# One scan over four rows instead of four scans: a change to the state-space stage of a macaron kernel

## The chip, the cores and the metric

The kernel runs on one core of one Trainium2 chip. The core has five engines that run side by side and meet at semaphores: TensorE (PE in the profile, its weight loads PEld), VectorE (DVE), ScalarE (ACT), GpSimd (POOL) and SyncE (SP), which here issues the DMAs. SBUF and PSUM are the on-chip memories, and all tiles here lie over up to 128 partitions. The kernel uses PSUM in banks of 512 fp32 per partition; TensorE's results go there, and no instruction of GpSimd in this kernel has an operand in it. The metric is the device time of one execution in microseconds.

## The reference

A macaron block over 2048 tokens of 128 features:

```
x = x + 0.5 * ffn(layernorm(x))
x = x + attn(layernorm(x))        # a state-space layer, in spite of its name
x = x + 0.5 * ffn(layernorm(x))
```

`ffn` is itself six layers, each of windowed attention (16 heads of 64, window 32) and a gated feed-forward part; it runs twice, with the same weights. The change lies in the middle line. There, with 256 channels d and 16 states n per channel,

```
delta = softplus(dt @ dt_w + dt_b)
dA  = exp(delta[l, d] * A[d, n])
dBu = (delta * u)[l, d] * B[l, n]
s   = dA[l] * s + dBu[l]            # in order of the tokens l, from s = 0
y[l, d] = sum over n of s[d, n] * C[l, n]
```

All data are fp32.

## The kernel before

The kernel works on the transposed activations, features on partitions. The attention layers go tile by tile (128 tokens), two segments of 1024 tokens, six layers, then the second run of `ffn`. The order of the instructions on each engine is written out by hand: `ORDER` gives for each stage of a tile a lag in steps and a place within the step, and `run` emits all the stages of a step in order of their place. Every engine executes its instructions in that order and waits where a semaphore is not yet there.

The state-space layer lies beside the attention tiles, from about 850 to 2550 us. It goes by pieces of 256 tokens (`SUB`), eight in all, one every 12 steps (`ROUND`), which is some 217 us. Its stages and their times in steps after the piece's start are listed in `SPACE`. Channels take two groups c of 128 partitions, and the 16 states n are taken in eight pairs q of two states j each, n = 2q + j. What runs per pair is

- `broadcast` (L1022): a DMA that spreads the rows of B and C of the two states over all partitions (tile `bc`);
- `source` (L1029): POOL computes `s` = B times delta u, in two instructions, one for each state (two SBUF inputs each, L1034);
- `decay` (L1039): ACT computes four exponentials of 256 elements into `da`, a tile of two PSUM banks laid out as [partition, j, c, 256 tokens] (L1044);
- `scan` (L1049): DVE runs four scans of 256 elements, one for each j and c, in place in `da`, with `da` as the factor, `s` as the addend and one column of `carry` as the initial value (L1055);
- `carried` (L1064): ACT copies the last column of each of the four rows into `carry`, for the next piece (L1066);
- `observe` (L1072): DVE multiplies `da` by C into `sc` (L1076);
- `gather` (L1084): PE adds the two rows of `sc` onto `y_ps` (L1089).

`s` and `bc` have two buffers each. `da` takes one of three pairs of PSUM banks that the attention tiles use too (`bank2`), from `decay` until `carried` and `observe` have both read it. `self.k.zero` (L1253 and L1254) is a column of zeros in SBUF, and `self.sp` the SBUF pool of this layer.

DVE's order around a scan is that of the tiles in the same step. The scans of a piece's first pair, for instance, are followed on DVE by the row sums of the softmax and their reciprocal (L546, L547), for which POOL's division L551 waits. Other stages that the text below names are the rotation on POOL (L408 adds two whole tiles, L440 multiplies a tile by a norm that is repeated over 64 elements), POOL's update of the activations of the piece before (L996), and small or plain DVE rows: L259 (a sum of 4 elements, one operand in PSUM), L631 (a memset of one column), L893 and L993 (256 elements, one operand in PSUM; L893 with a scalar for each partition).

Of the kernel before, what the change touches and what calls it, by code (L numbers as in the profile page):

```python
# [9 lines left out]
F32 = mybir.dt.float32  # L10
BF16 = mybir.dt.bfloat16
AF = mybir.ActivationFunctionType
ALU = mybir.AluOpType
# [4 lines left out]
P = 128  # L18
# [102 lines left out]
class Stream:  # L121
# [926 lines left out]

    def scan(self, b, s, q):  # L1049

        da = getattr(b, f"da{q}")
        for j in range(2):
            for c in range(2):
                n = 2 * q + j
                self.nc.vector.tensor_tensor_scan(  # L1055
                    da[:, j, c],
                    da[:, j, c],
                    getattr(b, f"s{q}")[:, j, c],
                    self.carry[:, c, n : n + 1],
                    ALU.mult,  # L1060
                    ALU.add,
                )

    def carried(self, b, s, q):  # L1064

# [312 lines left out]
```

## Time and profile before

| what | us |
|---|---|
| median of 3 runs | 3321.47 (3318.79 to 3322.2) |
| the profiled execution's own time | 3318.65 |
| its span in the profile | 3316.7 |
| PE busy | 3207.2 (97%) |
| POOL busy | 2907.3 (88%) |
| DVE busy | 2802.8 (85%) |
| ACT busy | 2551.6 (77%) |
| the 256 scans (L1055), all on DVE | 193.2 |

The mean granted clock of TensorE is 0.996. A row of the profile names a line of the kernel, the engine and operation, what is written and read, the shapes, how often, the busy time in us and the mean duration in ns, then how long the engine stood idle just before, and what ended most of that. In a timeline, a row has its start in us from the start of the span, its length in us, and in brackets an idle time ahead of it. The chain of waits is found backwards from the last instruction: at every step to what released it, or to the instruction before it on its engine.

### The profile page before, as it was taken

How to read it: one execution, taken by the hardware profiler on the slowest of the kernel's cores; microseconds unless marked ns; L12 is line 12 of the kernel's file. 1: busy time of each engine (PE TensorE's matmuls, PEld its weight loads, DVE VectorE, ACT ScalarE, POOL GpSimd, SP SyncE). 2: the span in 40 equal slices, each digit the busy share in tenths (PEclk: the TensorE clock that was granted, in tenths of full speed). 3: DMA queues.
4: the chain of work that ended last, by engine and by line, in shares of the span. 5: the costliest groups of instructions: out<-in, count | busy, mean ns of one | idle time of the engine just before them, and what ended most of it. 6: DMA issues, size and time to landing. Idle time of an engine off the chain costs nothing.

```text
span 3316.7 us, 97481 instructions
## 1 busy us (share of the span) xinstructions
PE 3207.2 (97%) x41936; PEld 2225.6 (67%) x41936; DVE 2802.8 (85%) x3540; ACT 2551.6 (77%) x4121; POOL 2907.3 (88%) x2317
## 2 busy tenths in 40 slices
PE   7999999999999999999999999999999999999997
PEld 4677677676666666666666666666666676777765
DVE  5778888887898989889989889898988888888884
ACT  6777777778778778787787877877777777777775
POOL 6999999998988989889888898898988888988983
PEclk9999999999999999999999999999999999999999
DMA  8222221221211122121211122111121111111000
GB/s 259 76 67 65 66 67 58 71 68 45 59 52 43 47 53 56 50 61 37 56 51 54 47 53 57 42 52 53 52 63 39 31 41 44 32 36 43 20 11 9
DMA packets 134494, 181.26 MB, mean 55 GB/s; under 512 B 13176, under 2 KB 91312, under 8 KB 127152
## 3 DMA queue, kind: packets, MB, share of 16 engines
q1 hardware_dynamic: 134064, 175.04, 18.0%
q8 instruction: 330, 5.41, 0.7%
q14 instruction: 100, 0.82, 0.1%
HBM read 138.75 MB, written 24.05 MB: 49 GB/s over the span
## 4 chain that ended last, share of the span: by engine, by line
PE 69%; DVE 12%; ACT 9%; POOL 7%; issue 2%; DMA 0%; SPq 0%; POOLq 0%; DVEq 0%; ACTq 0%
PE x_ps L372 16%; PE y_ps L617 16%; PE z_ps L596 8%; PE t_ps L453 8%; PE s_ps L511 6%; PE g_ps L698 3%; PE o_ps L744 3%; PE a_ps L698 3%; DVE da L1055 2%; DVE rot L391 2%; POOL rot L440 2%; DVE t L398 2%; PE y_ps L1089 2%; ACT da L1044 1%; ACT sq L384 1%
## 5 line engine op out<-in xcount | busy, mean ns | idle before, releaser
L408 POOL TENSOR_TENSOR rot<-rot,t 128x1024 f32<-128x1024 f32 x384 | 900.7, 2368 | 10.6 <-DVE rot L391 6.1
L372 PE MATMUL x_ps<-qk,r 128*128 128x512 f32 x1536 | 753.4, 613 | 29.6 <-ACT zt L608 10.1
L617 PEld LDWEIGHTS y_ps<-zt,m 128*128 128x128 f32 x6144 | 715.1, 192 | 63.8 <-ACT xc L667 36.6
L440 POOL TENSOR_TENSOR rot<-rot,rn 128x1024 f32<-128x1024 f32 x384 | 722.4, 1902 | 14.4
L617 PE MATMUL y_ps<-zt,m 128*128 128x128 f32 x6144 | 718.6, 275 | 5.3 <-ACT xc L667 3.1
L384 ACT ACTIVATE sq<-x_ps 128x1024 f32<-128x1024 f32 x384 | 393.2, 1024 | 276.3 <-DVE rot L391 229.9
L398 DVE TENSOR_TENSOR t<-x_ps,tab 128x1024 f32<-128x1024 f32 x384 | 467.7, 1218 | 154.6 <-PE i_ps L568 84.4
L551 POOL TENSOR_TENSOR pr<-pr,rs 128x1024 f32<-128x1024 f32 x192 | 365.2, 1902 | 198.8 <-DVE rs L547 174.0
L372 PEld LDWEIGHTS x_ps<-qk,r 128*128 128x128 f32 x1536 | 271.7, 190 | 361.8 <-issue 232.8
L391 DVE TENSOR_TENSOR rot<-x_ps,tab 128x1024 f32<-128x1024 f32 x384 | 467.3, 1217 | 20.0 <-ACT sq L384 19.5
L608 ACT COPY zt<-z_ps 128x1024 f32<-128x1024 f32 x384 | 368.9, 1010 | 140.8 <-PE z_ps L596 140.6
L414 DVE TENSOR_REDUCE ss<-sq 128x16 f32<-128x1024 f32 x384 | 466.5, 1215 | 7.7 <-ACT sq L384 5.0
L596 PE MATMUL z_ps<-pt,xw 32*128 32x512 f32 x3072 | 402.5, 614 | 3.1 <-DVE t L398 1.4
L535 POOL TENSOR_TENSOR pr<-pr,mx 128x1024 f32<-128x1024 f32 x192 | 365.3, 1903 | 25.9 <-ACT carry L1066 19.4
L453 PE MATMUL t_ps<-cs,rot 128*128 128x128 f32 x3072 | 370.9, 273 | 4.3 <-DVE sc L1076 2.1
L453 PEld LDWEIGHTS t_ps<-cs,rot 128*128 128x128 f32 x3072 | 344.1, 141 | 32.7 <-issue 9.8
L511 PE MATMUL s_ps<-kt,qt 64*32 64x64 f32 x24576 | 287.3, 225 | 0.5 <-issue 0.5
L511 PEld LDWEIGHTS s_ps<-kt,qt 64*32 64x32 f32 x24576 | 255.9, 105 | 47.1 <-issue 46.0
L541 ACT ACTIVATE pr<-pr 128x1024 f32<-128x1024 f32 x192 | 203.2, 1058 | 106.9 <-POOL pr L535 106.1
L596 PEld LDWEIGHTS z_ps<-pt,xw 32*128 32x128 f32 x3072 | 146.6, 184 | 163.4 <-issue 129.6
L561 DVE STREAM_TRANSPOSE pt<-pr 128x1024 f32<-128x1024 f32 x192 | 237.0, 1234 | 2.3 <-POOL pr L551 2.3
L546 DVE TENSOR_REDUCE rs<-pr 128x16 f32<-128x1024 f32 x192 | 232.9, 1213 | 6.2 <-ACT pr L541 3.3
(144 smaller groups left out, 4809.0 us busy)
## 6 DMA issues: line engine op xcount, KB each, us to landing
bc<-bc SPq DMA_DIRECT2D x64, 512.0 KB, 5.4
tab<-tab SPq DMA_DIRECT2D x120, 256.0 KB, 2.6
qk<-in_wqk_dram SPq DMA_DIRECT2D x24, 1024.0 KB, 5.0
m<-m SPq DMA_DIRECT2D x24, 1024.0 KB, 5.3
tab<-in_tabs_dram SPq DMA_DIRECT2D x48, 256.0 KB, 2.9
xw<-xw SPq DMA_DIRECT2D x192, 48.0 KB, 3.3
m<-mst SPq DMA_DIRECT2D x6, 1024.0 KB
w<-w1s SPq DMA_DIRECT2D x18, 341.0 KB, 3.5
```

The lines of the kernel that those rows point to most:

```text
L372: nc.tensor.matmul(out=x[:, j], lhsT=self.columns(g), rhs=st.w.qk[:, bass.ds(kind * INNER + j * 512, 512)], start=True, stop=True,)
L384: self.nc.scalar.activation(st.sq[kind], st.x[kind], AF.Square)
L391: self.nc.vector.tensor_tensor(st.rot[kind], st.x[kind], cos, ALU.mult)
L398: self.nc.vector.tensor_tensor(st.t2[kind].rearrange("p h (two c) -> p h two c", two=2), st.x[kind].rearrange("p h (two c) -> p h two c", ...
L408: self.nc.gpsimd.tensor_tensor(st.rot[kind], st.rot[kind], st.t2[kind], ALU.add)
L414: self.nc.vector.tensor_reduce(st.ss[:, kind, :], st.sq[kind], AX.X, ALU.add)
L440: self.nc.gpsimd.tensor_tensor(st.rot[kind], st.rot[kind], st.rn[:, kind, :].unsqueeze(2).to_broadcast([P, HEADS, DH]), ALU.mult,)
L453: self.nc.tensor.transpose(t_ps[:, c, :], flat[:, bass.ts(c, P)], self.k.ident)
L511: nc.tensor.matmul(out=st.s[32 * b : 32 * b + 32, par, c, :], lhsT=st.qt[rows, c, bass.ts(b, WIN)], rhs=st.kt[rows, c, bass.ds(WIN * b, 2 ...
L596: self.nc.tensor.matmul(out=st.z[b // 2][:, b % 2].rearrange("p (h q) -> p h q", q=WIN), lhsT=st.xw[rows, j, :], rhs=st.pt[rows, :, j, :], ...
L608: self.nc.scalar.copy(st.zt[:, 2 * half : 2 * half + 2].rearrange("p b h q -> p b (h q)"), st.z[half])
L617: self.nc.tensor.matmul(out=st.y_ps.rearrange("p (b q) -> p b q", q=WIN), lhsT=st.w.m[:, h // 2, h % 2, :], rhs=st.zt[:, :, h, :], start=( ...
```

## The change

`scan` computes the same states with one scan over all four rows of the pair, 1024 elements laid end to end. So that no row runs on into the next, the first column of `da` (the four decays at the first token of each row) is multiplied by the carry into a small new tile (4 elements per partition), that product is added to the first column of the source `s`, and the first column of `da` is set to zero; the scan then takes a constant zero as its initial value. All four instructions are DVE's, where the four scans stood. The sum into the source has both of its inputs in SBUF, `s` and the small tile; the product has one in PSUM and one in SBUF. On the other engines the instructions and their order are the same. In place of the waits of the four scans (the first and the third each waited for one half of the source from POOL, the first for the decays from ACT), the product waits for the decays, and the sum for both halves of the source.

```diff
     def scan(self, b, s, q):
 
-        da = getattr(b, f"da{q}")
-        for j in range(2):
-            for c in range(2):
-                n = 2 * q + j
-                self.nc.vector.tensor_tensor_scan(
-                    da[:, j, c],
-                    da[:, j, c],
-                    getattr(b, f"s{q}")[:, j, c],
-                    self.carry[:, c, n : n + 1],
-                    ALU.mult,
-                    ALU.add,
-                )
+
+        nc, da, src = self.nc, getattr(b, f"da{q}"), getattr(b, f"s{q}")
+        first, tmp = da[:, :, :, 0], self.sp.tile([P, 2, 2], F32, tag="s0", name="s0")
+        carry = self.carry[:, :, 2 * q : 2 * q + 2].rearrange("p c j -> p j c")
+        nc.vector.tensor_tensor(tmp, first, carry, ALU.mult)
+        nc.vector.tensor_tensor(src[:, :, :, 0], src[:, :, :, 0], tmp, ALU.add)
+        nc.vector.memset(first, 0.0)
+        flat = da.rearrange("p j c t -> p (j c t)")
+        nc.vector.tensor_tensor_scan(
+            flat, flat, src.rearrange("p j c t -> p (j c t)"), self.k.zero, ALU.mult, ALU.add
+        )
```

## The prediction

> **What bounds the kernel now.** First the page's busy shares and its chain, then busy time by stretch, then the chain of waits within the stretch that holds the scans, then the rows that give prices, last the timeline around single scans.
>
> ```profile
> PE 3207.2 (97%) x41936; PEld 2225.6 (67%) x41936; DVE 2802.8 (85%) x3540; ACT 2551.6 (77%) x4121; POOL 2907.3 (88%) x2317
> PE 69%; DVE 12%; ACT 9%; POOL 7%; issue 2%; DMA 0%; SPq 0%; POOLq 0%; DVEq 0%; ACTq 0%
> ...
> 850.00:2550.00 1700.00, 1646.15 (x20661) 1121.60 (x20660) 1524.77 (x1934) 1348.77 (x2253) 1513.85 (x1209) 1.00 0.19 51
> ```
>
> TensorE (PE) bounds the whole. All scans lie between 857 and 2542 us, so the third line (length, then busy PE, PEld, DVE, ACT, POOL) is the one to reason with: in 1700 us PE idles 54 us, DVE 175 us, POOL 186 us. No change to DVE can gain more than those 54 us. But PE there waits now and then for chains that run through DVE:
>
> ```profile
> by line: PE x_ps L372 13.5%; PE y_ps L617 11.2%; PE z_ps L596 6.4%; PE t_ps L453 6.0%; DVE da L1055 4.5%; PE s_ps L511 4.2%; PE y_ps L1089 3.0%; DVE rot L391 3.0%; issue 2.9%; DVE t L398 2.9%; ACT da L1044 2.7%; DVE ss L414 2.3%; POOL rot L
> ```
>
> 4.5% of 1700 us is 76.9 us of scans on the chain that ended last. Counting its pieces by pair, 26 of the 64 pairs of states are on it. With a pair called by its place q = 0 to 7 in its piece of 256 tokens: six of place 0, five of place 1, four of place 2, seven of place 3, two of place 5 and one each of places 6 and 7. The other 38 pairs have slack.
>
> **What goes.** The four scans of each pair.
>
> ```profile
> L1055 DVE TENSOR_TENSOR_SCAN da<-da,carry,s 128x256 f32<-128x256 f32 x256 | 193.2, 755 | 12.1 <-POOL s L1034 1.8
> L1076 DVE TENSOR_TENSOR sc<-da,bc 128x1024 f32<-128x1024 f32 x64 | 78.2, 1222 | 3.2 <-PE y_ps L1089 1.4 <-issue 0.2
> L893 DVE SCALAR_TENSOR_TENSOR u<-u_ps,pv,u 128x256 f32<-128x256 f32 x48 | 22.5, 482 | 7.7 <-ACT u L881 6.6
> L993 DVE TENSOR_TENSOR xm<-o_ps,xm 128x256 f32<-128x256 f32 x8 | 3.4, 424 | 0.2
> L259 DVE TENSOR_TENSOR b<-b_ps,pv 128x4 f32<-128x4 f32 x6 | 1.0, 163 | 9.5 <-PE b_ps L248 9.5
> L631 DVE MEMSET r<- 64x1 f32 x12 | 0.7, 59 | 0.7
> ...
> 1074.02 3.21 DVE L1055 TENSOR_TENSOR_SCAN da<-da,carry,s 128x256 f32<-128x256 f32 x4 [0.23 <-POOL s L1034]
> 1077.14 1.19 DVE L546 TENSOR_REDUCE rs<-pr 128x16 f32<-128x1024 f32 x1
> ...
> 1092.83 3.19 DVE L1055 TENSOR_TENSOR_SCAN da<-da,carry,s 128x256 f32<-128x256 f32 x4
> 1095.93 0.96 DVE L758 SCALAR_TENSOR_TENSOR r<-o_ps,pv,r 64x256 f32<-64x256 f32 x2
> ```
>
> From the first scan's start to the next instruction's start DVE is taken 3.12 and 3.10 us in these two; the mean of all 64 in the timeline is 3.08 us.
>
> **What comes, without any new wait.** The long scan: two-tensor rows of 256 and 1024 elements (424 and 1222 ns) give 1.04 ns per element and 158 ns fixed; a per-partition scalar adds 58 (482 against 424). The scan has one, so 216 of its 755 ns are fixed and 539 are 256 elements, 2.11 ns each. 1024 elements: 216 + 2156 = 2.37 us. Its scalar is now a constant zero, also a pointer, so the 216 stay. Product of first decay and carry (PSUM by SBUF, 4 elements): 0.16 by L259. Sum into the source: 0.16, the same row. The zeroing: 0.06 by L631; 0.16 if PSUM makes it cost what L259 does, nothing if it runs under the sum. Two waits on DVE's own semaphore at 0.03 each (1198.06 + 1.22 to 1199.31 from L546 to L547 in the timeline). The next instruction starts 0.09 before the scan's end, as now. Together 0.16 + 0.03 + 0.16 + 0.06 + 0.03 + 2.37 - 0.09 = 2.72, so 0.36 us less per pair (0.26 to 0.42).
>
> **A wait that is moved forward.** Now the third scan alone needs the second half of the source; the sum, which stands ahead of the whole long scan, will need both. Place 0 pays: POOL writes both halves from 1072.71 to 1075.21, DVE starts its scan at 1074.02, when the first is done. The sum can start at 1075.24, and the next instruction at 1075.24 + 0.16 + 0.06 + 0.03 + 2.37 - 0.09 = 1077.77 instead of 1077.14: 0.63 us more, in 7 of the 8 pieces (in the last, POOL ends 0.09 after the scan's start, and the pair gains like the others). Behind it on DVE stand the row sums L546 and L547, which POOL's L551 waits for, and then the product L1076 that PE's L1089 waits for. In the other 56 pairs both halves are done 0.35 us or more before the scan starts, and all four decays of ACT end ahead of the first scan in all 64, so the waits for whole tiles cost nothing there. The carry is 200 us old. No queue other than DVE's changes an instruction; no DMA is added or moved.
>
> Over all pairs DVE saves 57 x 0.36 - 7 x 0.63 = 16.1 us. On the chain: 20 x 0.36 - 6 x 0.63 = 3.4 us less. Off it the gain goes into DVE's idle time.
>
> **The sum's two operands.** Every two-tensor instruction of DVE in this trace takes one tensor from PSUM; the new sum into the source reads both from SBUF. The trace has no such row on DVE. POOL, whose instructions all read SBUF, is busy 1513.85 of the 1700 us, and often without a gap:
>
> ```profile
> 1091.18 1.29 POOL L1034 TENSOR_TENSOR s<-bc,du 128x512 f32<-128x512 f32 x1
> 1092.41 4.69 POOL L408 TENSOR_TENSOR rot<-rot,t 128x1024 f32<-128x1024 f32 x2
> ...
> L408 POOL TENSOR_TENSOR rot<-rot,t 128x1024 f32<-128x1024 f32 x384 | 900.7, 2368 | 10.6 <-DVE rot L391 6.1 <-DVE t L398 4.5
> L440 POOL TENSOR_TENSOR rot<-rot,rn 128x1024 f32<-128x1024 f32 x384 | 722.4, 1902 | 14.4
> ```
>
> L408 reads two whole tensors and takes 2368 ns; L440, one of whose operands is repeated, 1902: what an instruction reads from SBUF costs POOL time. So the sum's price has two ends. Low: 0.16 us, as costed. High: it stands until the POOL instruction then running ends. I read that remainder 0.2 us after each scan's start (place 0: after the second half) from the timeline: means by place 0.85, 1.59, 1.71, 0.12, 0.57, 1.82, 0.48, 0.66 us, 62.3 us over 64 pairs, 26.6 us over the 26 on the chain. At 1092.83 + 0.2, for instance, the first L408 of the fence has 1.77 us left. I take the high end, at somewhat better than even: the rows nearest to an instruction with both tensors in SBUF are POOL's, not DVE's rows with one in PSUM, and those show reads of SBUF to be what POOL's time goes into. Then the chain gets 26.6 - 3.4 = 23.2 us longer. DVE's work over all pairs would grow by 62.3 - 16.1 = 46.2; I count the other 23.0 us, off the chain, as lying in DVE's 175 us of idle time, and if that cover is gone the time grows by the 46.2.
>
> POOL's durations beside a busy DVE hardly move (L408: 2339 to 2398 ns over 384), as is to be expected where no DVE instruction reads two SBUF tensors. The Trainium skill (SBUF — State Buffer, "Who interferes with whom") speaks against the change: a VectorE instruction with two SBUF inputs shares its second read interface with GpSimd, and whichever issues second is blocked until the first is done. By that rule the time grows by 23 to 46 us, by the low end it falls by 3 to 16 us; no run here shows it yet.
>
> **Sum.** The profiled execution took 3318.65 us (span 3316.7), 2.8 below the median of 3321.47. 3318.65 + 23.2 = 3341.9; against the median, 3345.
>
> **Rivals.**
> (a) The sum waits for nothing: 3.4 to 16.1 us faster, 3305 to 3318. For it: it reads four elements per partition, and DVE's rows have never been held up by POOL. Against it: it is the first to need two reads of SBUF. This is the case on the other side. It decides at a mean wait of 3.4 / 26 = 0.13 us on the chain: below that the change isn't slower.
> (b) The sum waits for more than one POOL instruction, since POOL's follow each other with no gap (L408's two take 4.69 us together). One further 1.9 us instruction on each chain pair adds 26 x 1.9 = 49 us: 3394.
> (c) The scan's 755 ns are mostly fixed. At 1.04 ns per element 256 of them are 266 and 489 fixed; the long scan would take 1.55 us, 0.82 less than costed, 21 us on the chain: 3324 with the wait, 3297 without. Against it: no other row has a fixed part above 216. At the other end, were everything proportional, the scan would take 3.02 us and the chain grow by a further 17 us.
>
> **How the numbers follow.** One wait for POOL: 0.52. Rival (a): 0.34. Rival (b): 0.10. Rival (c): 0.04. About 0.2% (6.6 us) is what a measurement of this kernel can tell from no change. (a) lies across -6.6 us, so I split it: 0.14 faster, 0.20 same; (c) adds 0.03 to faster and 0.01 to same; of the first case nothing worth a number is within 6.6 us. Faster 0.17, same 0.21, slower 0.62. The range: from 3308, which leaves out the lower part of (a) and (c) without the wait, up to 3372, the 46.2 us with 4 more for the dearer zeroing (3321.5 + 50), which leaves out most of (b). The likeliest case's own range is 3335 to 3372.
>
> **What would show it.** The sum's row (into s, 128x4): near 0.16 us means (a), a mean near 1 us with a wide spread, or idle time ahead of it that ends with POOL's instruction, means the forecast. The long scan's row at 2.37 us; 1.55 or 3.0 would prove that step wrong. The product and the zeroing at 0.16 and 0.06. In place 0 the sum should wait for POOL's second half. PE's idle time in 850 to 2550 us should rise from 54 to near 77 us. It is wrong if POOL lets four elements pass at once.

## The result, and the profile after

The changed kernel takes 3354.86 us (median of 4 runs, 3353.51 to 3356.85) against 3320.18 us for the kernel before (4 runs): a ratio of 1.0104, 95% interval 1.0087 to 1.0122, or 34.7 us more. The span of its profiled execution is 3354.2 us, 37.5 more than before; 2.2 of these had come before the first scan, where both kernels are the same.

The page of the changed kernel, its busy shares and the chain by engine; then busy time from 850 to 2550 us (length, then PE, PEld, DVE, ACT and POOL, clock, DMA):

```profile
PE 3222.4 (96%) x41936; PEld 2233.7 (67%) x41936; DVE 2837.9 (85%) x3540; ACT 2557.5 (76%) x4121; POOL 2910.4 (87%) x2317
PE 67%; DVE 17%; POOL 8%; ACT 5%; issue 3%; DMA 0%; POOLq 0%; DVEq 0%; SPq 0%; ACTq 0%
...
850.00:2550.00 1700.00, 1626.58 (x20234) 1106.18 (x20233) 1526.96 (x1894) 1327.22 (x2209) 1489.13 (x1190) 0.99 0.18 50
```

DVE is on the chain for 17% of the span instead of 12%, and PE idles 73 us in the stretch instead of 54 (in this stretch of the slower kernel it also gets through 427 fewer matmuls). Over the whole execution PE idles 131.8 us instead of 109.5, and the same 41936 matmuls keep it busy 3222.4 us instead of 3207.2, at a mean granted clock of 0.993 instead of 0.996. So of the 37.5 us, 22.3 are idle time of PE and 15.2 are longer busy time. No run separates the two, and what a wait costs in time below contains both.

The groups of the changed kernel's four new instructions say where DVE's time went:

```profile
L1059 DVE TENSOR_TENSOR_SCAN da<-da,zero,s 128x1024 f32<-128x1024 f32 x64 | 150.9, 2357 | 2.2
L1056 DVE TENSOR_TENSOR s<-s,s 128x4 f32<-128x4 f32 x64 | 65.3, 1020 | 14.3 <-POOL s L1034 10.1
L1055 DVE TENSOR_TENSOR s<-da,carry 128x4 f32<-128x4 f32 x64 | 9.6, 150 | 0.5
L1057 DVE MEMSET da<- 128x4 f32 x64 | 4.0, 62 | 0.7
```

The scans cost 42.3 us less than the 193.2 of before. The sum of four elements, both of whose tensors are in SBUF, costs 65.3 us, with a mean of 1020 ns; the product, one of whose tensors is in PSUM, costs 150 ns. Row by row the sum takes 166 to 2301 ns. The timeline around one of them, a pair of place 2 (start, length; rows of DVE and POOL alone):

```profile
1148.07 4.70 POOL L408 TENSOR_TENSOR rot<-rot,t 128x1024 f32<-128x1024 f32 x2
...
1151.05 0.16 DVE L1055 TENSOR_TENSOR s<-da,carry 128x4 f32<-128x4 f32 x1
1151.25 1.55 DVE L1056 TENSOR_TENSOR s<-s,s 128x4 f32<-128x4 f32 x1
1152.80 0.06 DVE L1057 MEMSET da<- 128x4 f32 x1
1152.86 0.28 POOL L421 TENSOR_SCALAR ss<-ss 128x32 f32<-128x32 f32 x1
1152.90 2.36 DVE L1059 TENSOR_TENSOR_SCAN da<-da,zero,s 128x1024 f32<-128x1024 f32 x1
```

The sum starts at 1151.25, within POOL's second L408, and ends at 1152.80, 0.03 us after that one has ended (1152.77). The wait doesn't show as idle time of DVE; it lies in the length of the sum's own row. And a pair of place 0, again DVE and POOL alone:

```profile
1081.20 2.50 POOL L1034 TENSOR_TENSOR s<-bc,du 128x512 f32<-128x512 f32 x2
...
1082.15 0.15 DVE L1055 TENSOR_TENSOR s<-da,carry 128x4 f32<-128x4 f32 x1
1083.67 0.72 POOL L996 TENSOR_TENSOR xt<-xt,xm 128x256 f32<-128x256 f32 x1
1083.74 0.68 DVE L1056 TENSOR_TENSOR s<-s,s 128x4 f32<-128x4 f32 x1 [1.43 <-POOL s L1034]
1084.36 2.34 POOL L408 TENSOR_TENSOR rot<-rot,t 128x1024 f32<-128x1024 f32 x1
1084.43 0.06 DVE L1057 MEMSET da<- 128x4 f32 x1
```

First DVE is idle for 1.43 us until both halves of the source are written, then the sum waits for L996, which POOL began 0.07 us ahead of it. The next POOL instruction, L408, is recorded from 1084.36 on, before the sum ends, but the sum goes ahead of it; in all 64 pairs no wait lasted into a second POOL instruction.

### The profile page after: what moved, and what is told of

Same layout as the page of the kernel before. It is cut to its first block, busy times and chain, and to the rows that moved or that the text cites. A ratio compares the mean times of both kernels' runs of the same rounds, so it can differ in the third digit from the quotient of the medians.

```text
span 3354.2 us, 97449 instructions
## 1 busy us (share of the span) xinstructions
PE 3222.4 (96%) x41936; PEld 2233.7 (67%) x41936; DVE 2837.9 (85%) x3540; ACT 2557.5 (76%) x4121; POOL 2910.4 (87%) x2317
## 4 chain that ended last, share of the span: by engine, by line
PE 67%; DVE 17%; POOL 8%; ACT 5%; issue 3%; DMA 0%; POOLq 0%; DVEq 0%; SPq 0%; ACTq 0%
PE x_ps L372 16%; PE y_ps L617 16%; PE z_ps L596 8%; PE t_ps L453 8%; PE s_ps L511 5%; PE g_ps L698 3%; PE o_ps L744 3%; PE a_ps L698 3%; DVE da L1059 3%; DVE rot L391 2%; DVE t L398 2%; POOL rot L440 2%; DVE s L1056 1%; DVE ss L414 1%; PE s_ps L500 1%
## 5 line engine op out<-in xcount | busy, mean ns | idle before, releaser
L408 POOL TENSOR_TENSOR rot<-rot,t 128x1024 f32<-128x1024 f32 x384 | 901.0, 2369 | 10.9 <-DVE rot L391 6.4
L551 POOL TENSOR_TENSOR pr<-pr,rs 128x1024 f32<-128x1024 f32 x192 | 365.5, 1904 | 219.5 <-DVE rs L547 197.1
L391 DVE TENSOR_TENSOR rot<-x_ps,tab 128x1024 f32<-128x1024 f32 x384 | 467.7, 1218 | 20.8 <-ACT sq L384 20.5
L546 DVE TENSOR_REDUCE rs<-pr 128x16 f32<-128x1024 f32 x192 | 233.0, 1213 | 6.2 <-ACT pr L541 3.3
```

What stands on the lines that cost most here:

```text
L391: self.nc.vector.tensor_tensor(st.rot[kind], st.x[kind], cos, ALU.mult)
L408: self.nc.gpsimd.tensor_tensor(st.rot[kind], st.rot[kind], st.t2[kind], ALU.add)
```

## Experiments

Theory: the sum waits for POOL's running instruction because it reads two tensors from SBUF. Rivals: the sum's length is only where something else shows, namely the waits for whole tiles or the long scan.

### e1_psum: the product stays in PSUM

```diff
-        first, tmp = da[:, :, :, 0], self.sp.tile([P, 2, 2], F32, tag="s0", name="s0")
+        first = da[:, :, :, 0]
...
-        nc.vector.tensor_tensor(tmp, first, carry, ALU.mult)
-        nc.vector.tensor_tensor(src[:, :, :, 0], src[:, :, :, 0], tmp, ALU.add)
+        nc.vector.tensor_tensor(first, first, carry, ALU.mult)
+        nc.vector.tensor_tensor(src[:, :, :, 0], first, src[:, :, :, 0], ALU.add)
```

> The changed kernel, but the product of first decay and carry is left in PSUM (in place, in the first column of the decays), so that the sum into the source reads one tensor from PSUM and one from SBUF. Theory (the sum waits for POOL's running instruction because both its tensors are in SBUF): the sum's row falls from a mean of 1.02 us to 0.16, with hardly a spread; a pair takes DVE 2.77 us as in the pairs of the changed kernel that did not wait, so DVE works 57 x 0.31 - 7 x 0.66 = 13 us less than before, and the time is 3 to 13 us below before. Rival (the growth comes from the waits for whole tiles or from the long scan, and the sum's length is only where it shows): the sum's row, or another row of the pair, stays long, and the time stays some 30 us above before.

Measured: 3322.03 us (11 runs) against 3319.92 for before (21 runs), ratio 1.0010 (1.0002 to 1.0019), 3 us above before. The groups of this kernel:

```profile
L1059 DVE TENSOR_TENSOR_SCAN da<-da,zero,s 128x1024 f32<-128x1024 f32 x64 | 150.9, 2358 | 2.3
L1056 DVE TENSOR_TENSOR s<-da,s 128x4 f32<-128x4 f32 x64 | 10.6, 166 | 14.4 <-POOL s L1034 9.8 <-DVE da L1055 0.5
L1055 DVE TENSOR_TENSOR da<-da,carry 128x4 f32<-128x4 f32 x64 | 10.3, 160 | 0.6
```

The sum falls from 1020 to 166 ns, and with it some 31 us of the 34.7 go. The waits for whole tiles and the long scan are still there, so the rival falls as the main cause. What was not expected is that nothing is gained against before: DVE is busy 1507.38 us of the 1700 between 850 and 2550 us instead of 1524.77, but PE 1646.14 instead of 1646.15.

### e3_sum_alone: the sum without the rest of the change

```diff
         da = getattr(b, f"da{q}")
+        tmp = self.sp.tile([P, 2, 2], F32, tag="s0", name="s0")
+        self.nc.vector.tensor_tensor(tmp, b.du[:, :, 0:2], b.du[:, :, 2:4], ALU.add)
         for j in range(2):
```

> The kernel before with its four scans, and ahead of each pair's scans one sum of 4 elements per partition with both tensors in SBUF (two parts of delta times u, into a tile that nobody reads). If the wait for POOL is the cause by itself: the sum's row has a mean of 0.8 to 1.0 us and a spread up to 2.3, DVE works some 60 us more, and the time grows by 28 us (chain of before alone) to 50 us (0.79 of the work). If the sum by itself costs what a small sum costs: 0.16 us, 64 x 0.19 = 12 us of DVE work, and a time within 0 to 9 us of before.

Measured: 3359.34 us, ratio 1.0119 (1.0106 to 1.0133), 39 us above before. The new row of this kernel, and its timeline in the pair of place 2 shown above (DVE and POOL alone, up to the sum):

```profile
L1053 DVE TENSOR_TENSOR s<-du 128x4 f32<-128x4 f32 x64 | 54.8, 856 | 0.0
...
1144.68 4.68 POOL L408 TENSOR_TENSOR rot<-rot,t 128x1024 f32<-128x1024 f32 x2
...
1147.56 1.83 DVE L1053 TENSOR_TENSOR s<-du 128x4 f32<-128x4 f32 x1
```

A sum that nobody reads, of two tensors that had long been there, ahead of the four old scans, costs as much as the whole change. It ends at 1149.39, 0.03 us after POOL's L408, and 55 of the 64 sums wait in this way, each to the end of the POOL instruction that ran when it started. So it is the two operands in SBUF that make the sum wait, and not data that are not there yet.

### e7_on_chain and e8_off_chain: where the waits count

Both take the sum from PSUM or from SBUF by pair and are complements of each other. Below, `ON` stands for a list of the numbers 8 s + q of the 26 pairs on the chain of before, with s the piece; e8_off_chain has `not in`:

```diff
-        first, tmp = da[:, :, :, 0], self.sp.tile([P, 2, 2], F32, tag="s0", name="s0")
+        first = da[:, :, :, 0]
+        tmp = self.sp.tile([P, 2, 2], F32, tag="s0", name="s0") if 8 * s + q in ON else first
...
-        nc.vector.tensor_tensor(src[:, :, :, 0], src[:, :, :, 0], tmp, ALU.add)
+        nc.vector.tensor_tensor(src[:, :, :, 0], tmp, src[:, :, :, 0], ALU.add)
```

> The sum with both tensors in SBUF in just those 26 pairs that the chain of before goes through; one tensor in PSUM in the other 38. In the changed kernel the sums of these 26 waited 20.8 us. Theory of the prediction (a wait on the chain counts in full): 21 us above the run with all sums from PSUM. Theory that any wait on DVE counts by some 0.65, wherever it is: 13.5 us above it.

> The complement: both tensors in SBUF in the 38 pairs that are not on the chain of before, whose sums waited 33.8 us in the changed kernel. Theory of the prediction (a wait off the chain goes into DVE's idle time): 0 to 3 us above the run with all sums from PSUM. Theory that any wait on DVE counts by some 0.65: 22 us above it.

Measured: e7_on_chain 3337.77 us, ratio 1.0059 (1.0044 to 1.0075), which is 16 us above e1_psum's 1.0010; its 26 sums waited 19.3 us, so a wait there counts 0.84. e8_off_chain 3335.31 us, ratio 1.0045 (1.0031 to 1.0059), 12 us above; its 38 sums waited 32.7 us and count 0.36. As the intervals show, each of the two differences is uncertain by some 6 us. Together they make 28 of the 31 us that the changed kernel lies above e1_psum. The two operands of the sum have changed places here, and the sums from SBUF wait as before, so their order is not the cause. The chain of before tells rightly which waits weigh most, but not that the others weigh nothing: neither theory holds alone. Even the lower end of e8_off_chain's interval is above the upper end of e1_psum's.

### e2_wait47: the waits of places 4 to 7

The same edit with `q >= 4` as the condition.

> The sum with one tensor in PSUM in the pairs of place 0 to 3 of every piece, and with both in SBUF in places 4 to 7. In the changed kernel the waits of places 4 to 7 add up to 28.8 us. Of these, 5.1 us are in the four pairs that the chain of before goes through. Theory that only pairs on that chain count: 5 us above the run with all sums from PSUM. Theory that nearly all DVE time counts (the changed kernel gave 34.7 us for 44 us of DVE time, 0.79): 0.79 x 28.8 = 23 us above it.

Measured: 3340.56 us, ratio 1.0064 (1.0048 to 1.0079), 18 us above e1_psum for 28.7 us of waits, of which 5.1 in pairs on the chain. The chain alone (5 us) is refuted here too. With the factors of the two runs above one gets 0.84 x 5.1 + 0.36 x 23.7 = 13 us. This difference too is uncertain by some 6 us, so that this much agrees; it leaves open how constant the two factors are.

### e4_no_carry: no product, no sum

```diff
-        first, tmp = da[:, :, :, 0], self.sp.tile([P, 2, 2], F32, tag="s0", name="s0")
-        carry = self.carry[:, :, 2 * q : 2 * q + 2].rearrange("p c j -> p j c")
-        nc.vector.tensor_tensor(tmp, first, carry, ALU.mult)
-        nc.vector.tensor_tensor(src[:, :, :, 0], src[:, :, :, 0], tmp, ALU.add)
+        first = da[:, :, :, 0]
```

> The changed kernel without the product and the sum: the first column is set to zero and the long scan runs, so the carry from one piece to the next is left out. A pair takes DVE about 2.37 us, 0.71 less than before, except that in place 0 the scan now waits for both halves of the source (0.45 more): 57 x 0.71 - 7 x 0.45 = 37 us less DVE work. If only the chain of before counts: 20 x 0.71 - 6 x 0.45 = 11.5 us faster than before. If nearly all DVE time counts, 29 us faster, which would take more than half of PE's 54 us of idle time.

This kernel leaves out the carry, so every piece starts from zero. Measured: 3316.55 us (10 runs), ratio 0.9989 (0.9980 to 0.9998), 4 us below before. Less work on DVE is worth far less than more work costs, less even than the 11.5 us that the chain alone promised. In this kernel's chain DVE has 6% left:

```profile
PE 74%; ACT 10%; POOL 8%; DVE 6%; issue 2%; DMA 0%; SPq 0%; POOLq 0%; DVEq 0%; ACTq 0%
```

### e5_psum_late and e6_before_late: the wait for the second half

e5_psum_late is e1_psum, and e6_before_late the kernel before, each with one more edit:

```diff
-    ("ss0", 5.050), ("sc0", 5.187), ("cy0", 5.290), ("cp0", 5.424), ("da1", 5.926),
+    ("ss0", 5.050), ("sc0", 5.200), ("cy0", 5.290), ("cp0", 5.424), ("da1", 5.926),
```

> All sums with one tensor in PSUM, and in place 0 the row sums of the softmax with their reciprocal (L546, L547; 1.45 us) go ahead of the pair's scan on DVE instead of behind it, so that the sum no longer stands waiting for the second half of the source (9.8 us of idle time over 7 pairs with the sums from PSUM alone). If that wait is what eats the 13 us that DVE saves: 5 to 10 us faster than with the sums from PSUM alone, that is 3 to 8 us faster than before. If DVE's saved time is worth nothing because other engines set the pace: within 3 us of it.

> The kernel before with its four scans, and in place 0 the same two rows moved ahead of the scans: what the reordering does by itself. The wait for POOL ahead of the first scan was 1.8 us in all, so within 3 us of before by either theory; a larger gain would say that the order, and not the shorter scan, is what the run of the last kernel shows.

Measured: e5_psum_late 3315.75 us (11 runs) against 3319.23 for before (21 runs), ratio 0.9986 (0.9977 to 0.9995); e6_before_late 3318.73 us, ratio 0.9997 (0.9988 to 1.0006). Against e1_psum's 1.0010 the reordering gains 8 us, uncertain by some 4, where the sum has to wait for both halves, and in the old kernel nothing that can be measured. The timelines of place 0 of the second piece, first with the sums from PSUM alone (e1_psum), then with the reordering too (e5_psum_late). Of the rows of DVE and POOL, those are shown that the comparison needs:

```profile
1073.55 2.50 POOL L1034 TENSOR_TENSOR s<-bc,du 128x512 f32<-128x512 f32 x2
...
1074.53 0.16 DVE L1055 TENSOR_TENSOR da<-da,carry 128x4 f32<-128x4 f32 x1
...
1076.09 0.17 DVE L1056 TENSOR_TENSOR s<-da,s 128x4 f32<-128x4 f32 x1 [1.41 <-POOL s L1034]
...
1076.43 2.36 DVE L1059 TENSOR_TENSOR_SCAN da<-da,zero,s 128x1024 f32<-128x1024 f32 x1
...
1078.70 1.20 DVE L546 TENSOR_REDUCE rs<-pr 128x16 f32<-128x1024 f32 x1
```

```profile
1073.95 2.51 POOL L1034 TENSOR_TENSOR s<-bc,du 128x512 f32<-128x512 f32 x2
...
1074.94 1.21 DVE L546 TENSOR_REDUCE rs<-pr 128x16 f32<-128x1024 f32 x1
1076.19 0.25 DVE L547 RECIPROCAL rs<-rs 128x16 f32<-128x16 f32 x1
1076.36 0.15 DVE L1055 TENSOR_TENSOR da<-da,carry 128x4 f32<-128x4 f32 x1
...
1076.62 0.17 DVE L1056 TENSOR_TENSOR s<-da,s 128x4 f32<-128x4 f32 x1
```

The 1.41 us of standing idle are filled with the row sums, which POOL's L551 waits for: L546 begins 0.99 us after POOL has begun the source instead of 5.15. In e6_before_late it begins as early (0.97 us, the mean of the seven pieces) and nothing measurable is gained, so the earlier row sums alone are not what e5_psum_late gains by. e5_psum_late is the version that beats both kernels, by 0.14% of before, with an interval that reaches from 0.05 to 0.23%.

## Why the prediction was right, point by point

**The long scan, the product, the zeroing.** Forecast 2.37, 0.16 and 0.06 us; measured 2.357, 0.150 and 0.062. The rows of other operations gave the fixed and the proportional part of a scan that had only one size in the trace. Rival (c) is out. A pair whose sum doesn't wait takes DVE 2.76 us in the changed kernel (seven of the eight pairs of place 3), against a forecast of 2.72. The 4 us for a dearer zeroing at the upper end of the range were not worked out (64 times 0.10 us would be 6.4); with 0.062 us measured they were not needed.

**The sum.** The mechanism was the likeliest case's: it waits until the running POOL instruction ends, and not for a second one, so rivals (a) and (b) are out for the changed kernel. The mean wait, the row's 1.02 us less the 0.17 of e1_psum, is 0.85 us; forecast 0.97. By place the measured waits are 0.71, 0.76, 1.58, 0.18, 0.47, 1.61, 0.65 and 0.87 us. Place 1 is the one far off (forecast 1.59): DVE, held up in place 0, comes later, when POOL's L408 is further on. Where DVE isn't held up there (e5_psum_late), POOL's running instruction has 1.4 to 2.1 us left when the sum of place 1 starts. Over all pairs 54.6 us instead of 62.3, over the 26 on the chain of before 20.8 instead of 26.6. The Trainium skill's rule (SBUF — State Buffer, "Who interferes with whom") agrees with these runs: the sum is blocked until the earlier instruction is done with two inputs in SBUF, 1020 ns, and is not with one in PSUM, 166 ns.

**The cover that failed.** The forecast of 23.2 us more against a measured 34.7 rests on a step that was wrong: that the waits off the chain lie in DVE's idle time. In e8_off_chain they cost 12 us. DVE's 175 us of idle time did not take them up. A part of the way is seen in POOL, which waits for the softmax's row sums (L546, L547) that a late DVE delivers late. Between 850 and 2550 us this wait has grown from the first of these lines in the kernel before to the second in the changed one (waits in total, times, longest):

```profile
POOL pr L551 <- DVE rs L547: 72.4, 41, 5.0
```

```profile
POOL pr L551 <- DVE rs L547: 94.6, 48, 5.6
```

And from e1_psum to e8_off_chain:

```profile
POOL pr L551 <- DVE rs L547: 62.1, 38, 4.9
```

```profile
POOL pr L551 <- DVE rs L547: 77.5, 41, 4.9
```

It is not the only way: in e2_wait47, 18 us above e1_psum, the same wait is no longer than there (61.6 us). By which engine each late pair reaches PE was not followed further and stays open.

**The gain that didn't come.** Without the sum's wait the forecast was 3.4 us less on the chain. e1_psum is 3 us above before, by its interval 1 to 6. Two terms of the forecast can be set beside its rows. A pair that waits for nothing saves DVE less: it takes 2.85 us on the mean of places 1 to 7 there, as the zeroing starts later, so that 0.23 us of the 3.08 of before are saved, and not 0.36. In place 0 the row sums begin 5.15 us after POOL has begun the source, where it was 4.43 in before (1077.14 less 1072.71), so 0.72 us later; forecast 0.63. With both, 20 x 0.23 - 6 x 0.72 = 0.3 us would be left of the 3.4. The rest, from 0.3 us less to 3 us more, is little more than the uncertainty, and its cause stays open. One rival is the clock: in the profiled execution e1_psum's PE idles 1.5 us less than in before and is busy 4.9 us longer, at a granted clock of 0.995 instead of 0.996. With the wait of place 0 filled, e5_psum_late lies 3.6 us below e6_before_late (0.9986 against 0.9997), uncertain by some 4; 26 x 0.23 = 6.0 would be the full count on the chain, so these two don't tell whether a saving there counts in full. e4_no_carry does: 4 us, uncertain by some 3, instead of 11.5, with DVE at 6% of the chain. Where DVE gets faster, the chain goes over other engines, and where it gets slower, over DVE (17%).

So the time came out within the range, and nearer to its upper half, because two errors pointed the same way: no cover for the waits off the chain, and no gain from the shorter scans. A third pointed against them: the waits on the chain were 5.8 us shorter than forecast. That the total lies within 10 us of the forecast is in part luck, for the same reasoning with the measured waits would have given 20.8 - 3.4 = 17.4 us more, half of the measured 34.7. Without any cover it would have given 54.6 - 16.1 = 38.5, which is nearer.

## What to carry to other kernels

Before adding a small DVE instruction beside a busy POOL, look at where its tensors lie: here the sum with one in PSUM took 166 ns whatever POOL ran, and with both in SBUF it waited for the POOL instruction that ran. A group whose mean is far above that of a like shape (1020 against 166 ns), with a wide spread and little idle time ahead of it, can be a wait inside the instruction. And the chain of waits priced lengthening better than shortening here: waits added on it counted 0.84 of their length, of 11.5 us taken away on it 4 were gained, and waits added off it still counted 0.36.

## What was not expected of the hardware

- Where it waited, the sum ended 0.02 to 0.03 us after the POOL instruction that ran when it started, also where the next POOL instruction was already recorded as begun, and POOL's rows didn't get longer for it (L408: 2368 ns before, 2369 after).
- A sum of four elements took up to 2.30 us (in place 0 of the first piece, where L408 had begun 0.07 us ahead of it).
- A zeroing of four elements in PSUM takes 62 ns, hardly more than one of one element in SBUF (59). Where the sum reads the same column in PSUM, the zeroing starts some 75 ns after the sum ends instead of 7, and a pair that waits for nothing takes 2.8 to 2.9 us instead of 2.76.
